# Changing the order of u and v fetches on GpSimd's queue in a fused four-layer graph network

## The chip, the cores and the metric

The kernel runs on one NeuronCore of a Trainium2 chip. The metric is device time in microseconds (us) of one execution, from the first to the last instruction and what lies around them; less is better. Engines are called as the profile calls them: PE is the tensor engine's matrix multiply and PEld its weight load, DVE the vector engine, ACT the scalar engine, POOL GpSimd, SP the sync engine, which here only issues DMAs. A small q behind a name is that engine's sequencer.

## What is computed

Sixty-four graphs of 256 nodes with 256 features go through four layers with one sparse 256 x 256 adjacency. Layers 0, 1 and 3 are the same function; layer 2 is an attention layer (shown cut).

```python
def _L0_gnn_ref(h_t, A_a, A_m, W1, b1, W2, b2, Wa, ba, Wm, bm, beta1, beta2, beta3):
    d = h_t.shape[-1]
    pre_u = jnp.einsum('bud,dk->buk', h_t, W1[:d])
    pre_v = jnp.einsum('bvd,dk->bvk', h_t, W1[d:])
    hidden = jax.nn.relu(pre_u[:, :, None, :] + pre_v[:, None, :, :] + b1)
    S = jax.nn.sigmoid(jnp.einsum('buvk,ko->buvo', hidden, W2)[..., 0] + b2[0])
    a_t = jnp.einsum('buv,bud->bvd', S * A_a, h_t)
    m_t = jnp.einsum('uv,bud->bvd', A_m, h_t) * h_t
    z_t = beta1 * h_t + beta2 * (jnp.einsum('bvd,de->bve', a_t, Wa) + ba) + beta3 * (jnp.einsum('bvd,de->bve', m_t, Wm) + bm)
    return z_t

def _L2_gnn_ref(data, bias1, W1, W2, b2, bias2):
    feats = jnp.einsum('bni,oi->bno', data, W1)
    f1 = jnp.einsum('bno,o->bn', feats, W2) + b2[0]
    logits = f1[:, :, None] + f1[:, None, :]
    coefs = jax.nn.softmax(jax.nn.leaky_relu(logits) + bias1, axis=-1)
    return jnp.einsum('bij,bjo->bio', coefs, feats) + bias2 + data
```

A score S is only needed where the adjacency has an edge. For an edge from u to v it needs the row pre_u of u and the row pre_v of v, their sum, a relu and a weighted sum over 256 features.

## The kernel before

**Units.** The kernel works on pairs of graphs. Two streams, a and b, each take every other pair (`stream`, L882), and each pair passes three layers with scores, L0, L1 and L3, with the attention between L1 and L3. One pair in one such layer is a *unit*. The units run in the order aL0, bL0, aL1, bL1, aL3, bL3, then the next pairs; there are sixteen such cycles, 96 units. Below, a unit's kind is named like this, stream and layer. `LAST` in the code is L3, `GNN[0]` L0 and `GNN[1]` L1.

**Two units at a time.** `beside` (L908) runs the scores of one unit (the heavy part) together with everything else of the other stream (the light part): what follows the previous scores (`after`, L877: `spread`, then `finish`), the attention where it is due, and `before` (L646) of its next unit. The light part is a generator whose yields say how many steps of the heavy part are to be put in at that point, so the order on PE, DVE and ACT is written out by hand. Each engine runs its own instructions in the order in which they stand.

**Tables.** `before` multiplies the features by W1. It copies the u half to `pu` (ACT) and adds the bias to the v half in `pv` (DVE), and as soon as half m of both graphs is there, SP stores it to two tables in device memory, `tableu` and then `tablev` (L677). At m = 0 it also draws up the unit's list of fetches (L679) and issues the first six of them (`AHEAD`, L43 and L682). The rest is issued when the unit's scores are begun (L731).

**Fetches.** Edges are put into blocks of 128. Some blocks are made on PE (`made`, L761: the rows are copied to `pre` by ACT, and a matmul with `pick` adds them into the PSUM tile `ga`). The others are fetched (`fetch`, L811; the DMA is on L824): an indirect DMA from POOL gathers the 128 rows of u of block f from `tableu` into `fetched[f]`, and a second one gathers the rows from `tablev` and adds them to what is there. Each moves 128 rows of 2 KB, for both graphs. The second must wait until the first has landed. Below they are called uf and vf, u0 and v0 for block 0. A further block of edges that fit nowhere else is `left` (index −1 in the lists), with rows half as long. `issue_after` ties each fetch to the one before it, so POOL issues them in the order of the list. A list entry is a pair (block, 0 for u or 1 for v).

```python
FETCHES = [(0, 0), (1, 0), (2, 0), (0, 1), (3, 0), (1, 1)]
FETCHES += [(-1, 0), (2, 1), (4, 0), (3, 1), (-1, 1), (5, 0), (6, 0), (4, 1), (7, 0), (5, 1), (6, 1), (7, 1)]
FETCHES_MORE = FETCHES[:-2] + [(8, 0), (6, 1), (9, 0), (7, 1), (8, 1), (9, 1)]
```

Units of the kinds aL3 and bL1 have ten fetched blocks and take `FETCHES_MORE`, 22 fetches (`more`, L642); the other four kinds have eight and take `FETCHES`, 18. The tiles for blocks 0 to 3 belong to a stream, those for blocks 4 to 9 and `left` are shared by both.

**Scores.** `got` (L780) takes the fetched blocks in the order 0, 1, 2 and so on: for each, DVE computes relu, product and sum of both graphs (`tile_scores`, L733; in the profile `junk<-fetched`). After block 3 come `left` and the early half of the scores (`rated_all(EARLY, 0)`: ACT makes `val`, DVE `rm`). After the last block `end` (L804) does the same for the late half. `spread` (L862) of that unit stands in the light part of the next: its matmuls `ps<-rm` need the late `rm` for their second half.

The lines L39 to L41 with the lists and the function `before` are what the diff touches.

Of the kernel before, what the change touches and what calls it, by code (L numbers as in the profile page):

```python
# [17 lines left out]
GNN = ("L0_gnn_", "L1_gnn_", "L3_gnn_")  # L18
LAST = GNN[2]
# [18 lines left out]

FETCHES = [(0, 0), (1, 0), (2, 0), (0, 1), (3, 0), (1, 1)]  # L39
FETCHES += [(-1, 0), (2, 1), (4, 0), (3, 1), (-1, 1), (5, 0), (6, 0), (4, 1), (7, 0), (5, 1), (6, 1), (7, 1)]  # L40
FETCHES_MORE = FETCHES[:-2] + [(8, 0), (6, 1), (9, 0), (7, 1), (8, 1), (9, 1)]  # L41

AHEAD = 6  # L43

# [18 lines left out]
def blk(c):  # L63
    return slice(c * P, (c + 1) * P)
# [37 lines left out]
def adj_seq_kernel(ctx: ExitStack, tc: tile.TileContext, a: dict, out: bass.AP):  # L102
# [399 lines left out]
    def few(stack):  # L502
# [139 lines left out]
        def more(st, l):  # L642

            return (st["side"], l) in (("a", LAST), ("b", GNN[1]))

        def before(st, l):  # L646

            hT = st["hT"]
            pu = one.tile([P, 2, 2, D], FP, tag="pu" + st["side"], name="pu")
            pv = one.tile([P, 2, 2, D], FP, tag="pv" + st["side"], name="pv")  # L650
            pre = one.tile([P, len(FAST), 2 * D], FP, tag="pre" + st["side"], name="pre")
            order = [(m, g) for m in range(2) for g in range(2)]
            if l == LAST:
                order = [(m, g) for g in range(2) for m in range(2)]

            beside = {LAST: [0, (0, 1), (0, 1), (0, 1)], GNN[1]: [0] + [(0, 1)] * 3, GNN[0]: [0, 0, (0, 2), (0, 1)]}[l]
            beside = dict(zip(order, beside))
            st["tables"] = [
                tables.tile([N, 2 * D], FP, tag="table" + t + st["side"], name="table" + t) for t in "uv"
            ]  # L660

            st["pu"], st["pv"], st["pre"] = pu, pv, pre
            if l != GNN[1]:
                st["own"] = one.tile([P, 2, 2, D], FP, tag="own", name="own")
            t = one.tile([P, FIRST, 2, D], FP, tag="fetched" + st["side"], name="fetched")
            st["fetched"] = [t[:, f] for f in range(FIRST)]
            for m, g in order:
                if l == LAST and (m, g) == (1, 0):
                    st["flip"](1)
                t = psum()  # L670
                for c in range(2):
                    mm(out=t, lhsT=hT[:, c, g, blk(m)], rhs=w1[l][:, c], start=c == 0, stop=c == 1)
                scalar.copy(pu[:, m, g, :], t[:, 0, :])
                vector.tensor_tensor(pv[:, m, g, :], t[:, 1, :], b1row[l], ALU.add)
                if g == 1:
                    for rows, x in zip(st["tables"], (pu, pv)):
                        nc.sync.dma_start(out=rows[blk(m)], in_=flat(x)[:, m])  # L677
                    if m == 0:
                        st["fetches"] = list(FETCHES_MORE if more(st, l) else FETCHES)  # L679

                        if numbered:
                            fetch(st, AHEAD)  # L682
                if l != GNN[1]:
                    vector.tensor_tensor(st["own"][:, m, g, :], t[:, 0, :], pv[:, m, g, :], ALU.add)
                if g == 1:
                    if m == 0:
                        rows_u(st, 0, 2, 0, 0)
                    rows_v(st, 4 - 4 * m, 2, 0)
                yield beside[(m, g)]
                if l == GNN[1] and (m, g) == (0, 1):  # L690
                    st["turn"](0)
                    yield 0, 1
                    st["turn"](1)
                    yield 0
            yield REST_OF_IT

            yield from mixed(st, l, later if past else None, (0,) if more(st, l) else (0, 1))

        def scores(st, l, placed):
# [30 lines left out]
            fetched = st["fetched"]  # L730
            fetch(st, len(FETCHES_MORE))  # L731

# [78 lines left out]
        def fetch(st, n):  # L811

            now, st["fetches"] = st["fetches"][:n], st["fetches"][n:]
            for f, x in now:
                rows = st["tables"][x]
                if f < 0:
                    to, ids = st["left"], (left_u, left_v)[x]
                    rows = rows.rearrange("n (g d) -> (n g) d", g=2)
                else:
                    to, ids = st["fetched"][f].rearrange("p g d -> p (g d)"), (ids_u, ids_v)[x][:, f : f + 1]  # L820
                    if f < FIRST:
                        rows = rows[blk(0)]
                with tc.issue_after(fetches[-1]) if fetches else nullcontext():
                    this = nc.gpsimd.indirect_dma_start(  # L824
                        out=to, out_offset=None, in_=rows, in_offset=bass.IndirectOffsetOnAxis(ap=ids, axis=0),
                        compute_op=(ALU.bypass, ALU.add)[x],
                    )
                fetches.append(this.ins)

        def rows_u(st, f, n, k, m):  # L830

            h = halves[k]
            scalar.copy(
                st["pre"][h, f : f + n],
                st["pu"][h, m].rearrange("p g d -> p (g d)").unsqueeze(1).to_broadcast([64, n, 2 * D]),
            )

        def rows_v(st, f, n, k):

            for n in range(f, f + n):  # L840
                i = FAST[n][2]
                scalar.copy(
                    st["pre"][halves[1 - k], n], st["pv"][halves[i % 2], i // 2].rearrange("p g d -> p (g d)")
                )
# [37 lines left out]
        def stream(side, starts):  # L882

            sts = [{"b": b, "side": side} for b in starts]
            load(sts[0])
            short = [before(sts[0], GNN[0])]
            for i, st in enumerate(sts):
                yield short, (st, GNN[0]), False
                yield [after(st, GNN[0]), before(st, GNN[1])], (st, GNN[1]), True
                yield [after(st, GNN[1]), attention(st), before(st, GNN[2])], (st, GNN[2]), False  # L890
                short = [after(st, GNN[2])]
                if i + 1 < len(sts):
                    load(sts[i + 1])
                    short = [halfway(after(st, GNN[2]), 4, before(sts[i + 1], GNN[0]), 2)]
            yield short, None, False
# [29 lines left out]
        past, numbered, fetches, later = [], [], [], []  # L925
# [119 lines left out]
```

## Time and profile before

| | |
|---|---|
| Median of 3 runs | 3469.57 us (3468.32 to 3470.26) |
| Profiled execution: its own time | 3468.32 us |
| Profiled execution: span | 3466.6 us |
| Granted TensorE clock, mean | 0.991 |
| Fetches from tablev, 832: POOL busy, mean of one | 1317.3 us, 1583 ns |
| Fetches from tableu, 832: POOL busy, mean of one | 843.7 us, 1014 ns |
| Queue q0 (POOL's fetches): bytes, share of the 16 DMA engines | 461.49 MB, 65.2% |
| Queue q1 (SP's stores and loads): bytes, share | 154.96 MB, 12.8% |
| DVE on fetched blocks, 1664 passes: busy, mean of one | 643.0 us, 419 ns |

All lines at L79 are recorded in one helper, so groups are told apart by the names of what they write and read (`out<-in`). "Idle before" a group is the time in which the engine had nothing to run just before these instructions, and the name behind the arrow is what ended most of it; "issue" stands where the profile shows no releaser. In a timeline a line begins with start and duration in us, then engine and instruction, and in brackets the idle time before it.

### The profile page before, as it was taken

Reading aid. Unit: us, or ns where it says so; the run is one execution under the profiler, and the core shown is the slowest. Engines: PE = TensorE matmul, PEld = TensorE weight load, DVE = VectorE, ACT = ScalarE, POOL = GpSimd, SP = SyncE. Lnnn points to the kernel's source line nnn. Section 1 sums busy time; section 2 is a strip of 40 time slices with the busy share of each in tenths; the row PEclk is TensorE's granted clock in tenths of the full one; section 3 lists DMA queues with packets and bytes.
Section 4 is the critical chain, followed back from the end, with each engine's and each line's share of the span. In section 5 each row is a group of like instructions: output and inputs, shape, how many; then the busy total and the mean of one; then the engine's idle time right before and its main releaser. Section 6 shows DMA issues by size and latency. Waiting matters only on the chain.

```text
span 3466.6 us, 48384 instructions
## 1 busy us (share of the span) xinstructions
PE 3361.7 (97%) x14200; PEld 2067.6 (60%) x14200; DVE 2639.6 (76%) x10523; ACT 1557.2 (45%) x2833; POOL 2416.1 (70%) x1882
## 2 busy tenths in 40 slices
PE   6999999999999999999999999999999999999998
PEld 3566565565656566565665656656565665656655
DVE  5777787777777777777777877777777777777776
ACT  2444444444444444444444444444444444444442
POOL 3767777677767767677677776777767676776765
PEclk7999999999999999999999999999999999999999
DMA  5788787877878778787787877878787787877875
GB/s 148 164 185 188 166 207 164 193 176 178 197 168 196 179 178 186 176 196 171 178 188 165 197 170 187 183 170 205 167 196 173 178 197 165 193 179 175 190 162 129
DMA packets 289070, 620.81 MB, mean 179 GB/s; under 512 B 39072, under 2 KB 56352, under 8 KB 288800
## 3 DMA queue, kind: packets, MB, share of 16 engines
q0 software_dynamic: 204800, 461.49, 65.2%
q1 hardware_dynamic: 82416, 154.96, 12.8%
q8 instruction: 115, 1.88, 0.2%
q10 hardware_dynamic: 1584, 1.20, 0.1%
q14 instruction: 155, 1.27, 0.1%
HBM read 500.06 MB, written 117.44 MB: 178 GB/s over the span
## 4 chain that ended last, share of the span: by engine, by line
PE 68%; POOL 9%; DMA 7%; issue 7%; DVE 6%; ACT 3%; ACTq 0%; POOLq 0%; DVEq 0%
PE ps L79 52%; PE ga L79 16%; POOL fetched L824 8%; DMA fetched<-tablev,ids_v 4%; DVE junk L79 3%; ACT pre L79 2%; DMA fetched<-tableu,ids_u 2%; DVE rm L79 1%; DMA tableu<-pu 1%; POOL left L824 1%; DVE sa L79 1%; ACT val L79 1%; ACT pu L79 1%; DVE own L79 0%; DVE pv L79 0%
## 5 line engine op out<-in xcount | busy, mean ns | idle before, releaser
L824 POOL DMA_INDIRECT fetched<-tablev,ids_v x832 | 1317.3, 1583 | 381.1 <-issue 257.0
L824 POOL DMA_INDIRECT fetched<-tableu,ids_u x832 | 843.7, 1014 | 547.1 <-DMA tableu<-pu 286.7
L79 DVE SCALAR_TENSOR_TENSOR junk<-fetched,L_gnn_w2row 128x256 f32<-128x256 f32 x1664 | 643.0, 419 | 171.3 <-DMA fetched<-tablev,ids_v 167.3
L79 PE MATMUL ga<-pre,pick 128*128 128x512 f32 x1408 | 723.5, 609 | 37.0 <-ACT pre L79 27.4
L79 PE MATMUL ps<-L_gnn_w,hT 128*128 128x512 f32 x1536 | 708.0, 598 | 5.7 <-DMA hT<-in_xT_dram 5.7
L79 DVE SCALAR_TENSOR_TENSOR junk<-ga,L_gnn_w2row 128x256 f32<-128x256 f32 x1408 | 538.3, 419 | 103.7 <-PE ga L79 92.2
L79 PEld LDWEIGHTS ps<-L_gnn_w,hT 128*128 128x128 f32 x1536 | 280.6, 191 | 323.7 <-issue 300.2
L79 ACT COPY pre<-pv 64x512 f32<-64x512 f32 x704 | 434.0, 616 | 72.6 <-DVE pv L79 49.3
L79 PE MATMUL ps<-sa,h 128*128 128x256 f32 x1536 | 363.7, 382 | 13.2 <-DVE sa L79 8.9
L79 PEld LDWEIGHTS ps<-sa,h 128*128 128x128 f32 x1536 | 292.5, 191 | 126.0 <-issue 68.5
L79 ACT COPY pre<-pu 64x1024 f32<-64x1024 f32 x352 | 361.6, 1044 | 8.0 <-DVE ids_v L79 0.6
L79 PEld LDWEIGHTS ga<-pre,pick 128*128 128x128 f32 x1408 | 249.2, 191 | 184.4 <-issue 91.3
L79 ACT COPY pu<-ps 128x256 f32<-128x256 f32 x384 | 142.8, 372 | 481.3 <-PE ps L79 430.8
L79 ACT ACTIVATE hb<-hT,L_gnn_zbias,scas 128x512 f32<-128x512 f32 x128 | 97.3, 807 | 477.9 <-DVE hT L79 354.5
L79 DVE TENSOR_TENSOR rm<-gva,val 128x256 f32<-128x256 f32 x768 | 280.1, 420 | 33.1 <-ACT val L79 24.2
L79 PE MATMUL ps<-adj,h 128*128 128x256 f32 x1280 | 297.2, 384 | 4.0 <-issue 4.0
L79 PEld LDWEIGHTS ps<-adj,h 128*128 128x128 f32 x1280 | 242.1, 191 | 73.7 <-issue 40.3
L79 DVE TENSOR_TENSOR pv<-ps,L_gnn_b1row 128x256 f32<-128x256 f32 x384 | 161.7, 421 | 134.5 <-ACT pu L79 125.6
L79 PEld LDWEIGHTS ps<-rm,gu 128*64 128x64 f32 x3072 | 175.1, 138 | 135.2 <-issue 50.3
L79 ACT COPY aT<-ps 128x512 f32<-128x512 f32 x192 | 112.4, 585 | 315.9 <-PE ps L79 284.6
L79 PE MATMUL ps<-rm,gu 128*64 128x128 f32 x3072 | 218.7, 281 | 23.0 <-DVE rm L79 22.6
L79 PE MATMUL ps<-aT,L_gnn_Wa 128*128 128x512 f32 x512 | 240.6, 592 | 0.0
(149 smaller groups left out, 4211.8 us busy)
## 6 DMA issues: line engine op xcount, KB each, us to landing
tableu<-pu SPq DMA_DIRECT2D x192, 256.0 KB
tablev<-pv SPq DMA_DIRECT2D x192, 256.0 KB
hT<-in_xT_dram SPq DMA_DIRECT2D x32, 512.0 KB
h<-in_x_dram SPq DMA_DIRECT2D x64, 256.0 KB
out_dram<-h SPq DMA_DIRECT2D x64, 256.0 KB
fetched<-tableu,ids_u POOLq DMA_INDIRECT x832
fetched<-tablev,ids_v POOLq DMA_INDIRECT x832
L_gnn_w<-in_L_gnn_W_dram SPq DMA_DIRECT2D x6, 256.0 KB
```

The lines of the kernel that those rows point to most:

```text
L79: self.last = getattr(self.engine, op)(*a, **k)
L824: this = nc.gpsimd.indirect_dma_start(out=to, out_offset=None, in_=rows, in_offset=bass.IndirectOffsetOnAxis(ap=ids, axis=0), compute_op=( ...
```

## The change

A second list, `APART`, has the same 18 entries in another order. Units of the kinds bL0 and aL1 take it in place of `FETCHES`; aL3 and bL1 take a `FETCHES_MORE` that is now made from it; aL0 and bL3 keep `FETCHES`. Among the first six, u0 u1 u2 v0 u3 v1 becomes u0 u1 v0 u2 v1 u3; further on, left-v and u5 change places. What is fetched, where to, and how many fetches go ahead is as before.

```diff
@@ -38,7 +38,10 @@
 FETCHES = [(0, 0), (1, 0), (2, 0), (0, 1), (3, 0), (1, 1)]
 FETCHES += [(-1, 0), (2, 1), (4, 0), (3, 1), (-1, 1), (5, 0), (6, 0), (4, 1), (7, 0), (5, 1), (6, 1), (7, 1)]
-FETCHES_MORE = FETCHES[:-2] + [(8, 0), (6, 1), (9, 0), (7, 1), (8, 1), (9, 1)]
+
+APART = [(0, 0), (1, 0), (0, 1), (2, 0), (1, 1), (3, 0)]
+APART += [(-1, 0), (2, 1), (4, 0), (3, 1), (5, 0), (-1, 1), (6, 0), (4, 1), (7, 0), (5, 1), (6, 1), (7, 1)]
+FETCHES_MORE = APART[:-2] + [(8, 0), (6, 1), (9, 0), (7, 1), (8, 1), (9, 1)]
 
@@ -676,7 +679,8 @@
                     if m == 0:
-                        st["fetches"] = list(FETCHES_MORE if more(st, l) else FETCHES)
+                        tight = (st["side"], l) in (("b", LAST), ("a", GNN[0]))
+                        st["fetches"] = list(FETCHES_MORE if more(st, l) else FETCHES if tight else APART)
 
                         if numbered:
```

## The prediction, made before the changed kernel was run

> **What bounds the kernel now.** I read the page first: busy time, then the chain that ended last, then the waits of POOL and of DVE, and last the timeline around unit changes.
>
> ```profile
> PE 3361.7 (97%) x14200; PEld 2067.6 (60%) x14200; DVE 2639.6 (76%) x10523; ACT 1557.2 (45%) x2833; POOL 2416.1 (70%) x1882
> ...
> PE 68%; POOL 9%; DMA 7%; issue 7%; DVE 6%; ACT 3%; ACTq 0%; POOLq 0%; DVEq 0%
> PE ps L79 52%; PE ga L79 16%; POOL fetched L824 8%; DMA fetched<-tablev,ids_v 4%; DVE junk L79 3%; ACT pre L79 2%; DMA fetched<-tableu,ids_u 2%; DVE rm L79 1%; DMA tableu<-pu 1%; POOL left L824 1%; DVE sa L79 1%; ACT val L79 1%; ACT pu L79 1%; DVE own L79 0%; DVE pv L79 0%
> ```
>
> The reader is to see that PE carries the time, but not alone: fetches (POOL) and their landings (DMA) hold about 16% of the chain. Followed in order of time, the chain leaves PE at a tableu store, runs through a whole unit's fetches to the last landing, and comes back to PE by DVE. So the fetch stream of some units is what ends last.
>
> POOL's waits, then DVE's (total, times, longest):
>
> ```profile
> POOL fetched L824 <- DMA tableu<-pu: 286.7, 61, 10.1
> POOL fetched L824 <- DMA fetched<-tableu,ids_u: 127.8, 118, 3.5
> ```
>
> ```profile
> DVE junk L79 <- DMA fetched<-tablev,ids_v: 167.3, 129, 3.1
> ```
>
> The first is slack: POOL waits for a table. The second is POOL waiting for a u fetch to land before the v fetch that adds to it. Here is the start of an aL1 stream (u0 u1 u2, v0, u3, v1, left):
>
> ```profile
> 335.83 0.98 POOL L824 DMA_INDIRECT fetched<-tableu,ids_u  x1 [4.83 <-DMA tableu<-pu]
> 337.13 0.96 POOL L824 DMA_INDIRECT fetched<-tableu,ids_u  x1 [0.32 <-issue]
> 338.39 0.95 POOL L824 DMA_INDIRECT fetched<-tableu,ids_u  x1 [0.30 <-issue]
> 340.10 1.70 POOL L824 DMA_INDIRECT fetched<-tablev,ids_v  x1 [0.76 <-DMA fetched<-tableu,ids_u]
> 342.10 0.97 POOL L824 DMA_INDIRECT fetched<-tableu,ids_u  x1 [0.30 <-issue]
> 343.38 1.53 POOL L824 DMA_INDIRECT fetched<-tablev,ids_v  x1 [0.30 <-issue]
> 345.21 0.98 POOL L824 DMA_INDIRECT left<-tableu,left_u  x1 [0.31 <-DVE junk L79]
> ```
>
> v0 starts 4.27 us after u0 began; three u fetches did not fill that, 0.76 us were idle. And the end of a bL1 unit:
>
> ```profile
> 409.37 0.42 DVE L79 SCALAR_TENSOR_TENSOR junk<-fetched,L_gnn_w2row 128x256 f32<-128x256 f32 x1 [0.33 <-DMA fetched<-tablev,ids_v]
> ...
> 410.74 0.31 ACT L79 ACTIVATE val<-raw,L_gnn_halfb 128x16 f32<-128x16 f32 x1
> ...
> 413.05 1.13 PE L79 MATMUL ga<-pre,pick 128*128 128x512 f32 x2 [2.33 <-ACT pre L79]
> ```
>
> The last block lands, DVE rates it, ACT makes val and only then copies pre, and PE waits 2.33 us for pre.
>
> **What the Trainium skill says.** "DMA: Bandwidth & Descriptors", section "Anatomy of one DMA — SWDGE (gpsimd) path": a DMA costs about 2.0 us plus bytes over 436 GB/s, mostly the receipt, and engines do not wait on semaphores; the issuing sequencer does. For 256 KB that estimates 2.6 us after generation; here u0's start to v0's start is 4.3 to 6.1 us, 1.0 of it generation, so the trace is longer. Same page, "Two DMAs through the same engine are not ordered": the dependent DMA must wait for the first's semaphore; the trace shows v0 doing so. "Perfetto Trace Analysis", section "DMA Instruction — SWDGE (GPSIMD)": a bar on POOL ends when the descriptors are written, not when the data have moved, which agrees (a u bar is 0.98 us, its landing 3.3 to 5 us after its start).
>
> **The change, part by part.** The orders of the two builds agree on PE, DVE, ACT and SP; only POOL's fetches are permuted, nothing is added or removed. Four kinds (bL0, aL1, bL1, aL3; 64 of 96 streams) go from u0 u1 u2 v0 u3 v1 to u0 u1 v0 u2 v1 u3, and later left-v and u5 change places.
>
> From POOL's timeline, DVE's reads of fetched and the DMA records (a fetch has landed at its sixteenth 4-byte packet), means over units 6 to 89, in us; "late" is DVE's start on a block after its landing, whose least value, 0.4, is no slack:
>
> ```
> kind  idle before u0  idle before v0  late, block 3  late, last block
> aL0        0.31            2.39            7.60           1.86
> bL0        0.30            2.14            1.29           1.71
> aL1        4.38            0.65            0.48           0.51
> bL1        2.80            1.15            9.87           0.70
> aL3        6.05            1.11            9.72           0.74
> bL3        5.31            0.95            7.09           1.51
> ```
>
> (1) *u2 moves behind v0.* A u fetch takes 0.98 + 0.30 of issue = 1.28 us. v0 waits for u0's landing, which u2 does not touch: in the stream that begins at 410.30, u0's 64 packets began 2.0 to 3.6 us after its start and u1's only from 3.8. So v0 starts when it did; its wait grows by 1.28 (aL1 0.65 to 1.9, bL0 2.1 to 3.4), and u2 then stands behind it as new work. v1 keeps its time too (v0, one u, v1 in both). Bounds: +1.28 where v0 waited, and at most v0's excess idle (0.35 to 1.84) gained if u2 itself held it up. I take +1.28.
>
> (2) *u3 behind v1.* With (1), everything from left-u on is 1.28 later. Queued behind the longer wait are all remaining fetches of the stream; SP's table stores are on another queue and do not move. v1 finds u1 landed (5.2 to 5.9 after u0; v1 issues at 7.5 or later).
>
> (3) *u5 ahead of left-v.* u5 ends up 0.57 earlier, left-v 1.28 + 1.28 = 2.56 later. DVE reads left 3.03 us after landing in aL1 (2.65 usable), more elsewhere: nothing, hidden by DVE's earlier blocks; without that cover 1.28 more in aL1.
>
> (4) *Where 1.28 shows.* **Last block**: bL0 has 1.3 of slack, and PE's matmul on the late half of rm starts 0.86 us after rm's end there, against −0.28 in aL0, where it waited, so another 1.1: nothing (without this cover, up to 1.28). aL1: 1.28 − 0.11, minus 0.36 in the half of units where PE starts on rm at 0.17 rather than −0.19: 0.8 to 1.17, I take 1.0. bL1: 1.28 − 0.30 = 0.98 (one unit with 3.6 raises that mean; mostly 1.2). aL3: 1.28 − 0.34 = 0.94. **Block 3**, in the middle: where DVE stalls there today by 0, 0.3, 0.6 or over 1.2, PE's matmuls of the next 8 us come 0.1, 0.6, 0.8, 1.1 us later than their steady distance. bL0 would newly stall 1.28 − 0.9 = 0.4: 0.4 for PE. aL1's lies on its own stream and is contained in its end. **Blocks 0 and 1** stall DVE up to 3 us in bL1 and aL3, and PE loses under 0.1 there: no cost now, no gain.
>
> (5) *How they add.* A stream starts before the unit ahead of it has ended (aL3's tableu was stored at 406.69, bL1's last block read at 409.37), so a delay at one unit's end moves the next stream but one. Ends of neighbouring units overlap instead of adding: per cycle of six units the larger path is aL1 + aL3, 1.0 + 0.94, about 2.0 us (bL0 + bL1 gives 1.4). Sixteen cycles: **32 us**. Carried through all 96 units by one rule (an end's shift is the larger of the last end's shift, and its stream's start shift plus 1.28 less this unit's own slack; a stream's start shifts with the end two units back) it is 31 us without block 3 and 43 with it. The profiled execution took 3468.32 (span 3466.6 and 1.7 around), so 3500; the median of the runs is 1.25 above it: **3501**.
>
> **Rivals.**
> *Hidden (15%).* PE and DVE have other waits (matmuls start some 4 to 6 us per unit later than their steady distance), and these could take up most of the shift; then a third of it stays, 11 us: 3480, or as little as 4: 3474. Against it: ends are tight in most aL1 and bL1 units.
> *Everything adds (10%).* If streams start later after each delayed end, bL0 0.4 + aL1 1.0 + bL1 1.0 + aL3 0.94 = 3.3 a cycle, 53 us: 3522.
> *Not slower (14%).* If the wait before v0 belongs to u2 in the DMA rings, v0 starts after u1 without it, streams shorten by 0.35 to 1.84, and ends gain what DVE waits there today, about 0.7 a cycle: −11 us, 3458. It decides from v0 starting more than 1.28 us earlier, counted from u0, than before. For it: many v0 waits name no releaser. Against it: where one is named, it is a u fetch, and u0's packets finish before u2's begin.
> That the change does nothing is excluded: the built order differs.
>
> **How the numbers follow.** Main case 61%, 3488 to 3515. The range 3472 to 3522 leaves out the gain and the far end of adding. Two runs of this kernel are told apart from about 0.2%, 7 us. Slower by more: 61 + 10 + half of hidden, 7 = 78%; within: 8 + 2 = 10%; faster: 12%.
>
> **What would show it.** Right: in the four kinds v0's start after u0 unchanged (4.3 to 5.8) and its idle time 1.28 longer; u-to-last-v about 1.28 longer; more DVE waiting on tablev fetches at block 3 of bL0 and aL1 and at last blocks; aL0 and bL3 as before. Wrong: v0 clearly earlier after u0, or streams longer with the cycle still 210.5 us (hidden).

## The result, and the profile after

The changed kernel takes **3483.09 us** (median of 6 runs, 3477.86 to 3493.67), the kernel before in the same session 3467.55 (6 runs, 3462.10 to 3470.26). The ratio is 1.0045, 95% interval 1.0032 to 1.0059: slower by 15.5 us. The forecast, 3501, was slower by about 31. The profiled execution took 3482.22 us, with a span of 3480.5, 13.9 more than before.

Busy time and the chain that ended last, from the page of the changed kernel:

```profile
PE 3366.3 (97%) x14200; PEld 2070.5 (59%) x14200; DVE 2642.5 (76%) x10523; ACT 1557.0 (45%) x2833; POOL 2411.8 (69%) x1882
...
PE 55%; DMA 15%; POOL 13%; issue 8%; DVE 7%; ACT 2%; POOLq 0%; ACTq 0%; DVEq 0%
PE ps L82 42%; PE ga L82 13%; POOL fetched L828 11%; DMA fetched<-tablev,ids_v 7%; DMA fetched<-tableu,ids_u 5%; DVE junk L82 3%; DMA tableu<-pu 2%; POOL left L828 2%; ACT pre L82 1%; DVE rm L82 1%; DVE sa L82 1%; DVE own L82 1%; ACT val L82 1%; ACT pu L82 0%; DVE pv L82 0%
```

No engine works much more than before. What grew is the share of the chain that lies on landings: DMA from 7 to 15%. In two further traces of the kernel before (`before_same_chip`, `before_again`, both below) it is 11 and 9%, in a second one of the changed kernel (`after_again`) 14%. POOL's share, 9 and 13%, is no clear change: those two traces of before have 13 and 10%.

The groups of fetches from the same page (busy, mean ns of one, then idle time before them and what ended most of it):

```profile
L828 POOL DMA_INDIRECT fetched<-tablev,ids_v x832 | 1318.7, 1585 | 461.7 <-DMA fetched<-tableu,ids_u 241.8
L828 POOL DMA_INDIRECT fetched<-tableu,ids_u x832 | 841.5, 1011 | 483.5 <-DMA tableu<-pu 233.7
```

A fetch costs POOL what it did (1583 and 1014 ns before); only what stands before it changed.

POOL's waits, DVE's wait for fetched blocks, and what PE waits for (total, times, longest):

```profile
POOL fetched L828 <- DMA fetched<-tableu,ids_u: 243.3, 151, 4.1
POOL fetched L828 <- DMA tableu<-pu: 233.7, 62, 6.2
```

```profile
DVE junk L82 <- DMA fetched<-tablev,ids_v: 192.0, 168, 3.1
```

```profile
PE ga L82 <- ACT pre L82: 41.8, 29, 2.4
PE ps L82 <- DVE rm L82: 25.5, 30, 5.5
```

POOL waits 115 us more for the u fetch that v0 adds to (127.8 before) and 53 less for a table: a little under half of the new waiting is paid out of time in which POOL used to stand before a stream. DVE waits 25 us more (167.3 before), and PE 17 more in its two lines, which were before:

```profile
PE ga L79 <- ACT pre L79: 27.4, 25, 2.3
PE ps L79 <- DVE rm L79: 22.6, 27, 6.0
```

These last two differences don't carry far by themselves: the two further traces of the kernel before have 210 and 196 us for DVE, and 65 and 51 for PE's two lines. PE's own starts tell the kernels apart better. Taking by how much its matmuls on `rm` and on `pre` start later than their steady distance (the median distance from the matmul ahead), the three traces of the kernel before have 119, 138 and 132 us in all, and two of the changed kernel 143 and 144. So PE loses 5 to 26 us there. The 13.9 us of span fit into that, but they are not accounted for to the us.

The start of an aL1 stream, the unit that was shown of before:

```profile
338.70 1.02 POOL L828 DMA_INDIRECT fetched<-tableu,ids_u  x1 [4.35 <-DMA tableu<-pu]
340.02 1.05 POOL L828 DMA_INDIRECT fetched<-tableu,ids_u  x1 [0.30 <-issue]
342.87 1.56 POOL L828 DMA_INDIRECT fetched<-tablev,ids_v  x1 [1.80 <-DMA fetched<-tableu,ids_u]
344.74 0.98 POOL L828 DMA_INDIRECT fetched<-tableu,ids_u  x1 [0.30 <-issue]
```

v0 starts 4.17 us after u0 (4.27 before), with 1.80 us of idle time ahead of it (0.76 before), and u2 stands behind it. Over units 6 to 89, worked out from the trace's fetches and SP's stores, means in us, before and after:

```
kind  v0 after u0   idle before v0  u0 to last v's end  table store to u0
bL0   5.80  5.58     2.14  3.19       30.35  31.37        12.07  11.90
aL1   4.33  4.36     0.65  2.02       28.99  30.54         5.22   4.56
bL1   4.88  5.00     1.15  2.69       36.32  37.87         5.01   4.37
aL3   4.78  4.69     1.11  2.29       36.64  37.92         2.84   2.90
```

The first three columns of pairs are as forecast. The last is not: in aL1 and bL1 the first fetch starts 0.65 us sooner after its table was stored. No step had that. Nor had any that bL3, whose order was kept, starts 0.82 us later after its store (2.71 us before, 3.53 after): its table lands 3.25 us after the store instead of 2.45, behind an aL3 stream that ends later. With only aL3 changed the first fetch of bL3 came at 3.30. The prediction had the stores unmoved and bL3 as before; what this costs was not measured apart.

### The profile page after: what moved, and what is told of

Same layout as the page of the kernel before. It is cut to its first block, busy times and chain, and to the rows that moved or that the text cites. A ratio compares the mean times of both kernels' runs of the same rounds, so it can differ in the third digit from the quotient of the medians.

```text
span 3480.5 us, 48256 instructions
## 1 busy us (share of the span) xinstructions
PE 3366.3 (97%) x14200; PEld 2070.5 (59%) x14200; DVE 2642.5 (76%) x10523; ACT 1557.0 (45%) x2833; POOL 2411.8 (69%) x1882
## 4 chain that ended last, share of the span: by engine, by line
PE 55%; DMA 15%; POOL 13%; issue 8%; DVE 7%; ACT 2%; POOLq 0%; ACTq 0%; DVEq 0%
PE ps L82 42%; PE ga L82 13%; POOL fetched L828 11%; DMA fetched<-tablev,ids_v 7%; DMA fetched<-tableu,ids_u 5%; DVE junk L82 3%; DMA tableu<-pu 2%; POOL left L828 2%; ACT pre L82 1%; DVE rm L82 1%; DVE sa L82 1%; DVE own L82 1%; ACT val L82 1%; ACT pu L82 0%; DVE pv L82 0%
## 5 line engine op out<-in xcount | busy, mean ns | idle before, releaser
L82 PEld LDWEIGHTS ps<-adj,h 128*128 128x128 f32 x1280 | 241.9, 191 | 73.2 <-issue 39.5
L82 PE MATMUL ps<-mT,L_gnn_Wm 128*128 128x512 f32 x512 | 240.6, 592 | 0.0
```

The lines of the kernel that those rows point to most:

```text
L82: self.last = getattr(self.engine, op)(*a, **k)
```

## The experiments

They were run in five sets, each on one chip together with runs of the kernel before. Every ratio is against those. No kernel here leaves any of the computation out; only the order of fetches, or the pads named, differ.

### First set: one kind at a time

```diff
-                        st["fetches"] = list(FETCHES_MORE if more(st, l) else FETCHES)
+                        first = APART if (st["side"], l) in ONLY else FETCHES
+                        st["fetches"] = first[:-2] + FETCHES_MORE[-6:] if more(st, l) else list(first)
```

with `ONLY` naming aL3, aL1, bL1 or bL0.

> The new order in aL3 units alone; the other five kinds keep the old one. Theory (shift, with two give-backs): an aL3 stream is 1.28 us longer, it starts from a table that is stored only after POOL has long been idle, so nothing is given back before its end; about 0.9 us a cycle, 16 cycles: +13 to +15 us (ratio 1.004). Rival (the stall of DVE at block 3 in the middle of aL1 and bL0 units is what costs): aL3 has 9 us of slack at block 3, so 0 us.

> The new order in aL1 units alone. Theory: without the longer bL0 stream ahead of it, aL1's table does not land sooner, so the full 1.28 less 0.1 to 0.4 of slack shows at its end: 0.9 to 1.1 us a cycle at that end; PE keeps it as far as bL1 does not end by its own stream: +8 to +16 us. bL1's table, stored 1.5 us before the last aL1 fetch and no longer together with it, lands about 0.6 us sooner after its store. Rival (block 3): also slower, +10 to +16 us, but bL1's table is then stored later, too, since the stall comes before it.

> The new order in bL1 units alone. Theory: the stream's 1.28 falls on an end that already waits for its own stream (DVE waits at blocks 7, 8 and 9 add up to 0.8 us a unit), and the following aL3 stream starts from its own table: up to 1.2 us at bL1's end, of which aL3's own stream end keeps what exceeds its slack of 0.3: +5 to +14 us. The rule of the prediction, carried unit by unit, gave 15 us for this kind. Rival (block 3): 10 us of slack there, 0 us.

> The new order in bL0 units alone. Theory: bL0's end has 2.4 us of slack, so nothing is lost there; its last fetch is issued about 1 us later than before, behind the store of aL1's table instead of ahead of it, so that table lands 0.6 to 0.9 us sooner (u0 of aL1 starts 4.4 rather than 5.3 us after the store), aL1's stream starts and ends sooner, and its end stops waiting: 0 to -6 us, faster if anything. Rival (block 3): DVE stalls 0.4 us more at block 3 of bL0 and PE with it, +6 us. The rule of the prediction gave +7.5 us.

Measured: aL3 1.0030 (1.0017 to 1.0042), aL1 1.0025 (1.0011 to 1.0039), bL1 1.0033 (1.0022 to 1.0044), bL0 0.9991 (0.9982 to 1.0001). Times 3478 us, the median of before in this set, that is 10, 9, 11 and −3 us. Single kinds cost less than step (4) had, 15 to 16 us for aL3, bL1 or aL1 alone (0.94, 0.98 or 1.0 times sixteen). Yet bL1, which had been counted as covered by the larger path through aL1 and aL3, costs as much as they do. The sum of the four is 0.79%, well above the 0.45% of all four together. Either the delays overlap or something is given back. (Each single version has its own kind's exchange of u5 and left-v in it.) A hint is in the traces: after only bL0 was changed, the first fetch of aL1, the next unit, came 4.74 us after its table's store (5.11 to 5.17 in the other three), and after only aL1, that of bL1 came at 4.84 (4.91 to 5.21).

### Second set: the delay alone, the exchange alone, and a filled start

`before_same_chip` is the kernel before, for its trace. `pad_four` keeps the old order and puts two memsets, 1.28 us of POOL's time, behind v1 of the four kinds. `swap_only` exchanges only u5 and left-v in them. `fill_all` starts the streams of all six kinds with u0 u1 u2 u3 v0 v1.

```diff
+                        if (st["side"], l) in PADDED:
+                            st["fetches"][AHEAD:AHEAD] = [None, None]
...
+                if it is None:
+                    with tc.issue_after(fetches[-1]):
+                        fetches.append(nc.gpsimd.memset(pad, 0.0).ins)
+                    continue
```

```diff
+SWAP = list(FETCHES)
+SWAP[10], SWAP[11] = SWAP[11], SWAP[10]
...
+FETCHES[3:6] = [(3, 0), (0, 1), (1, 1)]
```

> The kernel before, unchanged, for a trace from the same chip as the three runs beside it. All theories: the time of before (3465 to 3480 us); POOL idle before v0 as in the trace shown (1.0 to 2.4 us by kind), 5.2 us from the store of aL1's tableu to its first fetch.

> The old order in all kinds, and in the four changed kinds two small memsets on POOL right behind v1 (about 0.64 us each with their issue, 1.28 in all): the shift without the reordering, and without a byte more in the DMA rings. Theory (only the 1.28 us by which the rest of the stream is later matters): the same loss as the change, +12 to +19 us, aL1's table landing sooner as there. Rival (the order itself matters: u2 and u3 behind the v fetches, or left-v behind u5): no loss, 0 to +5 us.

> In the four changed kinds only u5 and left-v change places; the first six fetches stay as before. Theory: left-v lands 1.28 us later with 2.7 us or more of slack, u5 sooner, nothing behind them moves: 0 us (within 4). Rival (the later left block delays the early half of the scores): +4 to +10 us, half of the change or more.

> The other direction, in all six kinds: u0 u1 u2 u3 v0 v1, so that one more u fetch stands in v0's wait. Theory: v0 starts at the later of its old time and 5.25 us after u0; the rest of the stream is sooner by what was idle before v0 up to 1.28: aL1 0.35, bL3 0.65, bL1 and aL3 0.8, bL0 and aL0 1.28. Ends wait for their streams in bL1 (0.8 us a unit), aL1 (0.4) and little in aL3 (0.1), so 0.3 to 0.8 us a cycle: -5 to -12 us. Rival (order itself, or DVE's stalls at blocks 0 and 1, which grow by up to 0.9 us in bL1 and aL3, matter): 0 to +10 us.

Measured: `pad_four` **1.0079** (1.0063 to 1.0094), `swap_only` **0.9971** (0.9961 to 0.9982), `fill_all` 0.9936 (0.9922 to 0.9949). The delay by itself costs 27 us of 3465, close to the 32 of the forecast and well above the 12 to 19 that I now expected; the exchange, costed at nothing, gains 10. The theory that delays are given back by tables that land sooner falls as the main cause: `pad_four` has later streams too, and costs more than the changed kernel did in the first result. (bL1's table does land sooner in it, 3.99 against 4.48 us after its store, aL1's doesn't, 4.47 against 4.39.) It is not quite the same delay: from u0 to the last v its streams are 0.67 to 1.12 us longer than in `before_same_chip`, where the change made it 1.02 to 1.55. `fill_all` gained 22 us where 5 to 12 were expected; it comes back below.

**Where the exchange gains.** Not in its own streams after the place of the exchange: from v3 to the last v they take 13.4 us in bL0 and 13.6 in aL1 in both kernels. It gains ahead of the *next* stream. Start of an aL1 stream in `swap_only`:

```profile
336.11 0.98 POOL L829 DMA_INDIRECT fetched<-tableu,ids_u  x1 [2.58 <-DMA tableu<-pu]
337.40 0.97 POOL L829 DMA_INDIRECT fetched<-tableu,ids_u  x1 [0.30 <-issue]
```

The line says only that the table ended the wait. The trace's semaphore events for this fetch (us), and those of the first line of before's aL1 stream above, tell how long after:

```
                       table landed   wait on its own      u0 starts
before (u0 at 335.83)     335.07      335.10 to 335.11      335.83
swap_only                 335.86      none                  336.11
```

and the instructions of the two built programs, for u0 of aL1 and for DVE's read of bL0's `left`:

```
before     POOL fetched<-tableu [waits DMAHW0, DMASW4]   DVE junk<-left [waits DMASW4, DVE]
swap_only  POOL fetched<-tableu [waits DMAHW0]           DVE junk<-left [waits DMASW5, DVE]
```

The reader is to see three things. Fetches take their semaphores in turn from a ring of eight (DMASW0 to 7), so u0 of a unit uses that of the fetch eight places back, and must know that one to have landed. Behind a unit of 18 fetches that place held left-v, for which no later fetch waits, so u0 got a second wait. It had been met some 12 us before, but u0 then carried that wait itself and the table's became an instruction of its own in front. With u5 in that place there is none, because v5 has waited for u5. And the price, from the fetches for which POOL had stood idle at least 0.5 us when the landing came, over the traces of these first two sets and of the two kernels: in 794 with one wait POOL started 0.26 us (tenth and ninetieth percentile 0.26) after the landing; in 272 with two whose first was the late one, 0.75 us (0.72 to 0.76). In 310 with two where the late one was the fetch's own, it was 0.26 us again, so it is not the number of waits that costs, but the late one standing in the instruction ahead. The exchange is worth 0.49 us at u0 of aL1 and at u0 of bL1. At u0 of aL0 and bL0, which also have it, POOL doesn't wait for the table. Ahead of aL3 and bL3 stands a unit of 22 fetches, and the eighth place back is u7, for which v7 has waited.

The Trainium skill, "Perfetto Trace Analysis", "Identifying Dependency Chains", says that an instruction that waits on several engines may get an instruction of its own ahead of it for the further conditions. That is what the trace shows here, for two semaphores of DMAs, with 0.49 us as its price on POOL.

### Third set: which unit's exchange counts, and whether the parts add up

`swap_early` exchanges in bL0 and aL1 alone, `swap_late` in bL1 and aL3, `first_only` has the changed first six without the exchange, `fill_swap` is `fill_all` with the exchange in bL0 and aL1.

```diff
+ONLY = (("b", GNN[0]), ("a", GNN[1]))
...
+ONLY = (("b", GNN[1]), ("a", LAST))
...
+APART = [(0, 0), (1, 0), (0, 1), (2, 0), (1, 1), (3, 0)] + FETCHES[6:]
```

> u5 and left-v change places in bL0 and aL1 only, the units ahead of aL1 and bL1; the first six fetches stay as before. Theory (a second wait): in the kernel before, u0 of aL1 and of bL1 waits for two semaphores, the table's and one that was met some 11 us earlier, by the landing of left-v of the unit ahead, eight fetches back; with two waits POOL starts 0.75 us after the table has landed, with one 0.26. The exchange puts u5 eight fetches back, whose landing v5 has already waited for, so the second wait goes. Then these two kinds carry the whole gain of the exchange: ratio 0.997 (-9 to -11 us), and u0 of aL1 and bL1 0.49 us after the table sooner. Rival (the exchange shortens the stream in which it is made): half of it, 0.9985 (-5 us).

> u5 and left-v change places in bL1 and aL3 only, the units ahead of aL3 and bL3. These fetch 22 times, so that eight fetches ahead of the next u0 stands u7, not left-v, and u0 of aL3 and bL3 has one wait in the kernel before. Theory (a second wait): no change, 0.9995 to 1.0005. Rival (the exchange shortens the stream in which it is made): half of the exchange's gain, 0.9985 (-5 us).

> The changed order of the first six fetches alone in the four kinds, without the exchange of u5 and left-v. Theory (shift as forecast, and the exchange gave a third of it back): as the kernel with POOL kept busy for as long behind v1, ratio 1.007 to 1.0085 (+24 to +30 us), u0 of aL1 and bL1 0.75 us after the table. Rival (what the changed kernel fell short by was never lost, the ends being hidden): as the changed kernel, 1.0045 (+15 us).

> u0 u1 u2 u3 v0 v1 at the start of every stream, and u5 and left-v exchanged in bL0 and aL1. Theory (a second wait): the two gains are of different kinds and add up: u0 of aL1 and bL1 still starts 0.75 us after the table with the filled start alone; 0.9936 x 0.9971 = 0.9907 (-32 us). Rival (ends of streams are no longer late once the start is filled, so an earlier start of aL1 and bL1 is hidden): 0.9935 (-23 us).

Measured: `swap_early` 0.9981 (0.9970 to 0.9993), `swap_late` 1.0000 (0.9985 to 1.0015), `first_only` 1.0085 (1.0061 to 1.0109), `fill_swap` 1.0165 (1.0143 to 1.0186). `swap_early` gained 7 us where 9 to 11 were expected. The times of the first two point to the second wait but would not exclude the rival, whose 0.9985 lies in both intervals. The traces do: u0 of aL1 and bL1 has one wait in all 28 streams of `swap_early` and starts 0.26 us after the table (median), two waits in all 28 of `swap_late`, and 0.75. `first_only` is as the theory said. `fill_swap` missed on the wrong side of one, by 2.6%.

### Fourth set: the filled start again

> The kernel before once more, for its trace on this chip: how long after PE's last matmul on rm DVE starts the step of sa that waits for it. On the chip of the filled start this was 0.1 us every time it waited; on the chip of the filled start with the exchange, and in the first trace of the kernel before, it was 0.4 to 3 us in some twenty of eighty waits. If that belongs to the chip, the three traces of this set agree with one another on whether such delays are there; if it belongs to the order of fetches, only the filled start with the exchange has them in number.

> The filled start u0 u1 u2 u3 v0 v1 in all kinds, once more beside the version with the exchange. Theory (the late hand-over from PE to DVE belongs to the chip): 0.9936 if no hand-over is late here, 1.000 to 1.015 if they are late as they were for the filled start with the exchange. Rival (the loss belongs to the exchange on top of the filled start): 0.9936 on any chip.

> The filled start with u5 and left-v exchanged in bL0 and aL1, once more. Theory (late hand-overs belong to the chip): 0.9907 if none is late here, 1.0165 if they are. Rival (the loss belongs to this order: streams so early that DVE arrives at the steps of the other unit ahead of PE): 1.0165 on any chip, and fill_all beside it at 0.9936.

Measured: `fill_all_again`, the same program as `fill_all`, **1.0178** (1.0161 to 1.0195); `fill_swap_again` 1.0102 (1.0078 to 1.0125). So the exchange is not to blame: the same filled start gained 0.6% in one set and lost 1.8% in another. What PE waits for in the two, first the second set's, then this one:

```profile
PE ga L82 <- ACT pre L82: 24.7, 32, 1.6
PE ps L82 <- DVE rm L82: 16.0, 20, 6.4
```

```profile
PE ps L82 <- DVE sa L82: 65.1, 45, 3.1
```

In the second set the waits for pre and rm shrank, as wanted (before_same_chip has 40.3 and 24.4). In the fourth there is a new first line, PE waiting for DVE's step `sa`, which isn't there at all in the other. DVE in turn, in the fourth set's trace:

```profile
419.14 0.42 DVE L82 SCALAR_TENSOR_TENSOR junk<-ga,L_gnn_w2row 128x256 f32<-128x256 f32 x1
419.49 0.08 DVE L82 DVE_READ_ACCUMULATOR junk<-ga,L_gnn_w2row 128x1 f32 x1
422.07 0.69 DVE L82 TENSOR_TENSOR sa<-sa,ps 128x512 f32<-128x512 f32 x1 [2.50 <-PE ga L82]
```

with, in all,

```profile
DVE sa L82 <- PE ga L82: 74.3, 38, 2.9
...
DVE sa L82 <- PE ps L82: 44.7, 53, 3.1
```

and PE:

```profile
418.68 1.09 PE L82 MATMUL ps<-rm,gu 128*64 128x128 f32 x16
419.71 1.12 PE L82 MATMUL ga<-pre,pick 128*128 128x512 f32 x2
420.67 0.59 PE L82 MATMUL ps<-sa,h 128*128 128x256 f32 x2
422.81 1.56 PE L82 MATMUL ps<-sa,h 128*128 128x256 f32 x6 [1.54 <-DVE sa L82]
```

`sa` needs the sixteen matmuls on rm, whose last ends at 419.77. DVE is free from 419.57 but starts `sa` at 422.07, and PE then stands until 422.81. Counted in each trace (DVE's waits before `sa`, how many started over 0.4 us after PE's last matmul on rm, the longest; and by how much PE's matmuls on `sa` start later than their steady distance, in all us):

```
trace                          waits  over 0.4  longest   PE on sa
second set, four kernels       72-81      0       0.1     1.1-1.5
before, first trace               82     36       3.1       19.5
before, fourth set                75     24       3.2        9.2
fill_all_again, fourth set        90     78       4.0      104.4
fill_swap, third set              91     87       4.8       92.5
fill_swap_again, fourth set       87     79       4.1       84.9
```

(The first expectation of this set speaks of some twenty late waits in eighty; counted as here it is 36 of 82 and, with the filled start and the exchange, 87 of 91.) Late hand-overs from PE to DVE are in every trace but those of the second set. Where they are, the kernel before has some too, mostly hidden; a filled start has two to over three times as many, and PE feels them. What PE loses on rm and pre shrinks all the same (by its starts, 95 to 100 us in the three filled starts of the table, 132 in `before_again`). The loss of the filled start goes with these hand-overs, and they are large enough for all of it: PE's matmuls on `sa` are late by 104 us in `fill_all_again` against 1 in `fill_all`, and the spans of these two executions differ by 98.5 us (3531.5 and 3433.0).

Two things in the traces narrow it down. In 622 of the 626 late hand-overs of all traces, PE's semaphore is recorded as raised less than 0.06 us before DVE starts (median 0.02). So DVE follows PE's signal at once, and what is late is that signal, counted from the end of the matmul, which the profile models. And it is this hand-over alone: of some 2500 other starts of DVE and ACT right behind a signal of PE, in the traces `before`, `fill_all_again` and `after_again`, one is over 0.25 us behind the last signalling matmul's end. Second, the traces with late hand-overs are the ones with gaps in their records: 79 to 85% of PE's semaphore updates are in them, against over 99.8% in the four of the second set. Whether the recording delays the signal, or one cause makes both, was not tested. The gaps also make the wait totals by releaser too low in all sets but the second, so these are best compared within one set.

### Fifth set: the change and its two parts on one chip

> The changed kernel, beside its two parts on one chip. Theory (shift plus exchange, whatever the chip): the ratio is the product of the two beside it, 1.0085 x 0.997 = 1.0055, and within its interval of 1.0032 to 1.0059. Rival (the filled start shows that earlier or later streams cost differently from chip to chip, so the first result does not carry over): a ratio outside 1.003 to 1.007, and not the product of the two.

> The first six fetches in the changed order in four kinds, without the exchange. Theory: 1.0085 as on the other chip, give or take 0.0015. Rival (chips differ): as the changed kernel beside it, or under 1.006.

> The exchange of u5 and left-v alone in four kinds. Theory (a second wait less at the first fetch of aL1 and bL1): 0.997 on any chip. Rival (as with the filled start, a gain from earlier streams shows only on a chip whose hand-overs from PE to DVE come in time): 1.000 or above if late hand-overs are in the trace.

Measured, beside a median of 3469.51 for before: the changed kernel 1.0066 (1.0045 to 1.0087), 3492.16 us; its first six alone 1.0098 (1.0076 to 1.0119), 3501.03; the exchange alone 0.9975 (0.9964 to 0.9985), 3461.57. In us, +31.5 and −7.9 make +23.6, and +22.7 was measured. This set ran on the chip of the second, by its number, and its traces do have late hand-overs (19 to 38 of 66 to 79, up to 3.5 us, 7 to 9 us for PE). So they are not bound to the chip, and the exchange is worth about as much with them as without (0.9975 and 0.9971).

DVE's and PE's waits with the first six alone:

```profile
DVE junk L82 <- DMA fetched<-tablev,ids_v: 250.3, 205, 3.0
```

```profile
PE ps L82 <- DVE rm L82: 47.8, 41, 5.7
PE ga L82 <- ACT pre L82: 40.2, 38, 2.0
```

and with the exchange alone:

```profile
DVE junk L83 <- DMA fetched<-tablev,ids_v: 173.5, 124, 3.4
```

```profile
PE ga L83 <- ACT pre L83: 27.9, 26, 2.3
PE ps L83 <- DVE rm L83: 24.2, 24, 6.5
```

The later streams reach PE by the path that the prediction followed, the last block and then rm and pre: 88 us of these two waits against 52. The changed kernel lies between, with 230.6 us for DVE and 73.2 for PE in this set. By PE's starts on rm and pre it is 165 us with the first six alone, 144 in the changed kernel and 124 with the exchange alone.

## Why the prediction went the right way and too far

(1) *u2 behind v0: right.* v0 kept its time after u0 (within 0.22 us in the four kinds), its wait grew by 1.05 to 1.54 where 1.28 was said, and the streams by 1.02 to 1.55. The rival in which v0's wait belongs to u2 is out: v0 would have started over 1.28 us earlier.

(2) *u3 behind v1, and everything from left-u on later: right.* `pad_four`, which delays the same fetches without reordering any, costs about as much as the first six alone: 1.0079 beside 1.0085 and 1.0098, intervals overlapping. That a delay is enough for such a loss is shown. That the order adds nothing to it is not, since the pads lengthen the streams by less (0.9 us on average against 1.35).

(3) *u5 ahead of left-v: **this step failed.*** It was costed at nothing because DVE's earlier blocks cover left-v. That part holds. What was overlooked is that the exchange changes which fetch stands eight places ahead of the next unit's u0, and with it whether u0 carries a second wait. It is worth −10 us (0.9971) and −8 (0.9975), in two sets. Taken from the 31 us of the forecast that leaves 21 to 24; measured were 22.7 in the last set and 15.5 in the first result (11 to 20 by its interval). So this step is the whole miss in the one and half to 60% of it in the other; why the first result is 7 us below the last is not shown, and their intervals overlap. The built programs, with the semaphores each instruction waits for, showed it without a run.

(4) *Where 1.28 shows: about right in sum, less so by kind.* A single kind costs less than its term: aL3 0.65 us a cycle (10.4/16) where 0.94 was said, bL1 0.72 for 0.98, aL1 0.54 for 1.0, with the exchange's gain at bL1 in it; bL0 alone, with the gain at aL1 in it, is near zero. DVE's stalls (means a unit, in us) are mostly at the forecast places:

```
                       before, three traces    changed, two traces
block 3 of aL1         0.49  0.76  0.65        1.14  1.28
block 3 of bL0         0.14  0.43  0.51        0.51  0.83
last block of aL1      0.42  0.41  0.41        0.76  0.95
last block of aL3      0.07  0.32  0.20        0.36  0.37
last block of bL1      0.23  0.33  0.28        0.19  0.20
```

The growth is clear in aL1, small beside the spread of the traces in bL0 and aL3, and absent in bL1, although its own stream is longer. The first fetch that starts sooner, step (3), is not the reason: without the exchange bL1 has 0.24 and 0.17 (the first six alone) and 0.26 (`pad_four`). So the 0.98 at bL1's last block did not show where it was forecast, and by which path bL1 alone costs 11 us stays open.

(5) *How they add: the sum was right, the rule isn't shown.* 32 us were forecast for the shift, 27 to 34 were measured, by the ratios (`pad_four`, `first_only`, `first_only_again`). But ends of neighbouring units were said to overlap, the path through aL1 and aL3 covering that through bL0 and bL1; bL1 alone costs 11 us, and the single kinds come close to adding: their 0.79% has the exchange's gain in it, so without it some 1.06%, 37 us (an estimate from 0.9971 and 0.9975). Smaller terms and more adding met in about the same sum. That the sum was so close is in part luck.

Of the rivals, *Hidden* (3480) is nearest in time and wrong in kind: the shift costs about what was said, and a quarter to a third of that is given back elsewhere. *Everything adds* (3522) was too much. *Not slower* named a mechanism that doesn't exist here; the gain that does exist, at u0, was in no case.

What stays open: why PE's signal to DVE comes up to 4.8 us late in most sets and never in one, with the same program. It goes with neither the order alone, nor the chip by its number, nor with what POOL is doing when the matmul ends: then POOL is in a v bar in 63% of the late cases, in a u bar in 13% and in a gap in 24%, against 62, 13 and 26% of the second set's waits, none of them late. It does go with gaps in the trace's semaphore records. It wasn't tried to take it apart further.

## What to carry to other kernels

A reordering of DMAs on one queue has two effects: what lies between an issue and its use, and which earlier DMA each one must know to have landed. The second is read from the waits of the built program, and one that is met long before still costs when it makes the late wait an instruction of its own. Of what was measured here, only the exchange alone beats both kernels in each set it ran in (0.9971, 0.9975); the filled start is a trap unless it is timed in more than one session.

## What the runs showed of the hardware that was not expected

- An indirect DMA on POOL starts 0.26 us after the landing it waits for, and 0.75 us when a second, long-met wait pushes the late one into an instruction ahead of it (794 and 272 cases); with two waits of which its own is the late one, 0.26 us as well (310 cases).
- The same program with a filled start took 3440.75 us in one set and 3528.98 in another (0.9936 and 1.0178 of before, whose own medians there are 3464.95 and 3465.78).
- DVE's step on `sa` can start up to 4.8 us after the matmul that it waits for has ended by the trace, while in one set it never took over 0.1 us. In the late cases it starts 0.02 us (median) after PE's semaphore is recorded as raised.
